# A two-layer graph transformer on one core: raw rows gathered in layer 2, and gathers that wait for the chunk two before

## The chip, the cores and the metric

One core of a Trainium2 chip runs the whole program in one launch. The metric is the time of one execution on the device in microseconds (us). A comparison gives the median of several runs; beside it one execution is recorded by the hardware profiler, and all stage times in this document are from such a record.

## The reference

A graph of N = 6250 nodes with D = 128 features and E = 106250 edges sorted by their target node. Two attention layers with 2 heads of 64, the same for both but for their weights:

```python
q, k, v = (h @ Wq + bq, h @ Wk + bk, h @ Wv + bv)         # per head
e = edge_attr @ We          # edge_attr: 64 message features and 32 cosines of a relative time
alpha = sum(q[dst] * (k[src] + e)) / 8
a = softmax of alpha over the edges of each target node
out = segment_sum((v[src] + e) * a, dst) + h @ Ws + bs
```

Between them h is normalised over the nodes (batch norm: mean and variance of each feature, then scale and shift), and a ReLU follows. Behind layer 2 the input x is added and each row goes through a layer norm.

## The kernel before, in words

**Chunks.** The edges are cut into 106 chunks of 1024 (8 tiles of 128), and a chunk's edges lead to at most 64 target nodes. `conv(c, extra)` works on them in a software pipeline: iteration k does different stages of chunks k+4 to k−2, written out by hand in a fixed order, and each engine keeps that order. `c` is 0 in layer 1 and 1 in layer 2.

**Rows.** For each chunk the source nodes' rows are gathered into a buffer `ff` (128 edges of a tile on the partitions, tiles side by side, followed by message features, time encoding and a few more columns). `gather(k)` (L751) issues 8 indirect DMAs of 128 rows each on GpSimd (POOL), which does nothing else in the loops. There are six such buffers, and in iteration k `fetch(k+4)` (plain loads on SP, and small DVE work) and `gather(k+4)` come first; so a chunk's gathers are issued four chunks ahead and wait only until the buffer of six chunks before is free.

**What happens to a chunk.** `turn_in` transposes its rows on TensorE (PE) in two halves (L805), and ScalarE (ACT) copies them from PSUM to `fft` (L812). All eight gathers of the chunk are awaited by its first transpose. In layer 1 the edge features are transposed too (L817, L818) and stored in `et_d` for layer 2; `encode` (L769 to L777) computes the time encoding on VectorE (DVE). `score` (L830, L831) multiplies with a table of the target nodes, `lowest` and `weigh` turn scores into exponentials (L837, L845), `turn_weights` transposes these (L855, L856), and `gather_sums` (L862) multiplies them with `ff`, which gives the weighted sums of rows and edge features, and the sum of weights in the last column. `divide` (L867 to L870), `finish_turn` (L882, L885), `apply` (L892 or L898, L899) and `finish` (L909 or L922 on) make the layer's output from these sums. The value and edge weights are applied to the sums, not to each edge; the table holds what the keys need.

**Extra work.** `pull(extra)` runs one or two steps of other work in each iteration: the tables of later blocks of 512 nodes (L629 to L639), and in layer 2 the residual of each block (L1085 to L1095). At the end of layer 1 it also turns finished blocks of h into rows and writes them to `h_d` (L1027, L1029, L1037), and takes their moments.

**Between the layers.** The moments give `scale` and `shift` (L1067 to L1076). Block 0 of h goes through the ReLU and gets its table. Then `conv(1, ...)` starts, and its first iteration calls `first_blocks`: the ReLU of the other twelve blocks in place (L1106), then each block is turned into rows again (49 transposes, 13 DVE copies) and written to a second table, `hn_d`. The first RAW = 3 chunks gather from `h_d`, raw, for which `fft` is made with a ReLU activation with scale and shift (L810) and `normalise` repairs `ff` in place with three DVE operations (L875, L876) before its sums; the other 103 chunks gather normalised rows from `hn_d`.

## Time and profile before

| | us |
|---|---|
| median of 3 runs | 2755.56 (2752.11 to 2757.98) |
| the profiled execution | 2730.3 |
| its span on the core | 2728.4 |
| PE busy in the span | 2340.9 (86%) |
| POOL busy | 1619.5 (59%) |
| DVE busy | 1342.3 (49%) |
| ACT busy | 1241.6 (46%) |
| mean granted TensorE clock | 0.952 |

The page shows the span of the profiled execution; what the execution takes beyond it lies before the first and behind the last instruction. Busy shares are means over stages: the preparation (to about 38 us, the first gather), layer 1 (to about 1390 us), the step between the layers and layer 2. In the timelines a row is one instruction, or several of one kind in a row (their count is behind the `x`); "remote" as the end of an idle time stands for something the record doesn't show. The bracket of a gather names what its queue waited for, "issue" that it waited for nothing visible.

### The profile page before, as it was taken

The page shows a single profiled execution, that of the slowest core. Times are in us where ns is not written, and L with a number is a line of the kernel's source. Part 1 is how long each engine was busy: PE and PEld are TensorE (multiplying, and loading weights), DVE is VectorE, ACT ScalarE, POOL GpSimd, SP SyncE. Part 2 cuts the span into 40 slices and gives each one's busy share as a digit, 9 for nine tenths or more (in the row PEclk, how much of TensorE's full clock was granted, in tenths as well). Part 3 has the DMA queues.
Part 4 walks back from the last instruction along what each step waited for, and adds up shares of the span by engine and source line. Part 5 has one row for each costly group of instructions (what it writes and reads, how often), then busy time and mean ns, then how long its engine had stood idle before and what let it go on. Part 6 is the DMA issues. An engine that isn't in the chain of part 4 may idle for free. (4 is left out here: it accounts for less than half of the span.)

```text
span 2728.4 us, 39114 instructions
## 1 busy us (share of the span) xinstructions
PE 2340.9 (86%) x11586; PEld 1725.5 (63%) x11586; DVE 1342.3 (49%) x4162; ACT 1241.6 (46%) x2167; POOL 1619.5 (59%) x1717
## 2 busy tenths in 40 slices
PE   5599999999898989888957998888898888888887
PEld 3366666767676767666734665666666666666655
DVE  5366666666666666666634333333333333333333
ACT  2366666665555555445522343333334333333344
POOL 3466666566666666666335666666666666666660
PEclk7799999999999999999978999998999999999998
DMA  6255555545555455555436554555555555544440
GB/s 205 80 177 145 154 164 149 150 131 161 160 151 158 130 163 154 142 150 149 119 106 175 157 154 144 147 156 155 152 153 142 159 151 152 156 135 129 137 135 27
DMA packets 241161, 396.59 MB, mean 145 GB/s; under 512 B 62609, under 2 KB 158094, under 8 KB 237614
## 3 DMA queue, kind: packets, MB, share of 16 engines
q1 hardware_dynamic: 167728, 239.73, 29.5%
q0 software_dynamic: 54656, 113.07, 16.2%
q10 hardware_dynamic: 18558, 41.20, 4.3%
q8 instruction: 98, 1.61, 0.2%
q14 instruction: 121, 0.99, 0.1%
HBM read 277.19 MB, written 113.17 MB: 143 GB/s over the span
## 5 line engine op out<-in xcount | busy, mean ns | idle before, releaser
L751 POOL DMA_INDIRECT ff<-xv_d,fsrcs x848 | 810.1, 955 | 512.8 <-issue 213.0
L751 POOL DMA_INDIRECT ff<-hn_d,fsrcs x824 | 782.2, 949 | 458.8 <-issue 208.7
L812 ACT COPY fft<-fpx 128x512 f32<-128x512 f32 x418 | 246.1, 589 | 1150.2 <-remote 439.9
L862 PE MATMUL fpa<-ff,fpt 128*128 128x225 f32 x3392 | 684.2, 354 | 0.6 <-issue 0.6
L862 PEld LDWEIGHTS fpa<-ff,fpt 128*128 128x128 f32 x3392 | 628.6, 190 | 4.8 <-issue 1.3
L830 PE MATMUL fps<-fft,ftab 128*128 128x512 f32 x848 | 480.4, 650 | 65.5 <-ACT fft L812 45.8
L837 DVE TENSOR_REDUCE flow<-fps 128x1 f32<-128x512 f32 x424 | 285.4, 686 | 455.5 <-PE fpx L805 124.5
L855 PEld LDWEIGHTS fppt<-fident,fs 128*128 128x128 f32 x1696 | 203.4, 145 | 145.2 <-issue 76.4
L856 ACT COPY fpt<-fppt 128x512 f32<-128x512 f32 x424 | 229.4, 585 | 108.8 <-PE fppt L855 47.5
L845 ACT ACTIVATE fs<-fps,fm 128x512 f32<-128x512 f32 x424 | 269.1, 689 | 4.8 <-DVE fm L839 2.1
L805 PE MATMUL fpx<-fident,ff 128*128 128x128 f32 x1696 | 259.3, 276 | 5.3 <-issue 1.1
L830 PEld LDWEIGHTS fps<-fft,ftab 128*128 128x128 f32 x848 | 168.0, 233 | 126.6 <-ACT fft L812 68.2
L855 PE MATMUL fppt<-fident,fs 128*128 128x128 f32 x1696 | 234.6, 282 | 11.6 <-ACT fft L810 5.4
L831 PE MATMUL fps<-fxT,ftab 112*128 112x512 f32 x424 | 236.8, 642 | 2.8 <-DMA fxT<-et_d 2.8
L831 PE MATMUL fps<-fet,ftab 112*128 112x512 f32 x424 | 221.0, 603 | 11.2 <-issue 11.2
L805 PEld LDWEIGHTS fpx<-fident,ff 128*128 128x128 f32 x1696 | 203.4, 142 | 34.8 <-issue 22.7
L817 PE MATMUL fpe<-fident,ff 128*112 128x128 f32 x848 | 133.4, 281 | 72.6 <-ACT fft L812 69.7
L831 PEld LDWEIGHTS fps<-fet,ftab 112*128 112x128 f32 x424 | 106.8, 252 | 91.0 <-issue 88.9
L831 PEld LDWEIGHTS fps<-fxT,ftab 112*128 112x128 f32 x424 | 90.7, 214 | 116.3 <-issue 111.0
L885 DVE COPY fat<-fpo 128x256 f32<-128x256 f32 x212 | 89.2, 421 | 138.9 <-remote 58.9
L817 PEld LDWEIGHTS fpe<-fident,ff 128*112 128x112 f32 x848 | 95.8, 136 | 88.9 <-ACT fft L812 83.3
L818 ACT COPY fet<-fpe 112x512 f32<-112x512 f32 x212 | 127.4, 601 | 45.1 <-remote 16.0
(203 smaller groups left out, 2402.4 us busy)
## 6 DMA issues: line engine op xcount, KB each, us to landing
fmsg<-in_edge_attr SPq DMA_DIRECT2D x212, 256.0 KB
et_d<-fet SPq DMA_DIRECT2D x106, 448.0 KB
fxT<-et_d SPq DMA_DIRECT2D x106, 448.0 KB
ftab<-tab_d SPq DMA_DIRECT2D x106, 192.0 KB
tab_d<-fo ACTq DMA_DIRECT2D x13, 1536.0 KB
ff<-xv_d,fsrcs POOLq DMA_INDIRECT x848
enc_d<-fzs SPq DMA_DIRECT2D x106, 128.0 KB
ftab<-tab_d SPq DMA_DIRECT2D x106, 128.0 KB
```

The costliest lines, as they stand in the source:

```text
L751: nc.gpsimd.indirect_dma_start(out=f[:, t, (1 if c else 0):1 + D], out_offset=None, in_=(h_d if k < RAW else hn_d) if c else pl.xv_d, in_o ...
L805: turn = nc.tensor.transpose(px[:, t * P:(t + 1) * P], s.f[:, u * 4 + t, 1:1 + D], ident)
L812: nc.scalar.copy(s.ft[:, u * GE:(u + 1) * GE], px)
L817: nc.tensor.transpose(pe[:EC, t * P:(t + 1) * P], s.f[:, u * 4 + t, 1 + D:], ident)
L818: nc.scalar.copy(s.et[:, u * GE:(u + 1) * GE], pe[:EC])
L830: nc.tensor.matmul(ps, s.tab[:, :, 0], s.ft[:, w], start=True, stop=False)
L831: nc.tensor.matmul(ps, s.tab[:EC, :, 1], s.et[:, w], start=False, stop=True)
L837: nc.vector.tensor_reduce(low[:, u:u + 1], s.ps[u], AX.X, OP.min)
L845: nc.scalar.activation(s.s[:, u * GE:(u + 1) * GE], s.ps[u], AF.Exp, bias=s.bias, scale=-1.0)
L855: nc.tensor.transpose(pp[:, t * P:(t + 1) * P], s.s[:, at:at + P], ident)
L856: nc.scalar.copy(s.pt[:, u * GE:(u + 1) * GE], pp)
L862: nc.tensor.matmul(s.pa, s.pt[:, t * P:(t + 1) * P], s.f[:, t, 1:1 + D + EW], start=t == 0, stop=t == T - 1)
```

## The change

1. `hn_d` and `first_blocks` are gone. All chunks of layer 2 gather raw rows from `h_d`, and `fft` is always made with the ReLU activation (L810).
2. `normalise(k)` runs for each chunk of layer 2, behind `finish_turn(k - 2)`, with two operations: multiply by the scale, and take the larger of that and minus the shift. That is the normalised row less the shift. As the weights of a node's edges add up to one, the missing shift is the same for each node after the division; its product with the value weights is added once to the last row of the edge weights `web[1]`, which meets the column of ones.
3. The ReLU of a block is done in `block(b0)`, when its table is made.
4. Gathers are paced. Chunks 0 and 1 are gathered at once. Chunk 2 waits for the second half of the transposes of chunk 0; chunk j from 3 on is issued behind the first half of the transposes of chunk j − 2 and waits for the last of these. In layer 1 that holds to chunk NEAR = 30; chunk 31 follows chunk 30 directly, and from 32 on gathers come at the start of an iteration, four chunks ahead, as before. In layer 2 it holds to the end.

```diff
-    RAW = 3
+    NEAR = 30
...
-        def gather(k):
+        def gather(k, step=None):
             f = ch[k].f
-            ch[k].rows = [
+            rows = ch[k].rows = [
                 nc.gpsimd.indirect_dma_start(
-                    out=..., in_=(h_d if k < RAW else hn_d) if c else pl.xv_d,
+                    out=..., in_=h_d if c else pl.xv_d,
...
+            if step is not None:
+                tc.add_manual_dep(rows[0].ins, step.ins.name, together, reason="gathers keep to the pace of the chunks")
...
-                turn = nc.tensor.transpose(px[:, t * P:(t + 1) * P], s.f[:, u * 4 + t, 1:1 + D], ident)
+                turn = s.step = nc.tensor.transpose(px[:, t * P:(t + 1) * P], s.f[:, u * 4 + t, 1:1 + D], ident)
...
-            if c and k < RAW:
+            if c:
                 nc.scalar.activation(s.ft[:, u * GE:(u + 1) * GE], px, AF.Relu, bias=pl.shift, scale=pl.scale)
...
         def normalise(k):
             rows = ch[k].f[:, :, 1:1 + D]
-            for i, op in enumerate((OP.mult, OP.add)):
+            for i, op in enumerate((OP.mult, OP.max)):
                 nc.vector.tensor_tensor(rows, rows, pl.spread[:, None, i].to_broadcast([P, T, D]), op)
-            nc.vector.tensor_scalar(rows, rows, 0.0, None, op0=OP.max)
...
                 if on(k + AHEAD):
                     fetch(k + AHEAD)
-                    gather(k + AHEAD)
-                if k == -AHEAD and c:
-                    first_blocks()
+                    if c == 0 and k + AHEAD > NEAR + 1:
+                        gather(k + AHEAD)
...
                 if on(k - 2):
                     finish_turn(k - 2)
+                if c and on(k):
+                    normalise(k)
                 if on(k + 1):
                     turn_in(k + 1, 0)
+                if on(k + 3) and k != -1 and (c or k + 3 <= NEAR):
+                    gather(k + 3, ch[k + 1].step if on(k + 1) else None)
+                    if c == 0 and k + 3 == NEAR:
+                        gather(k + 4)
                 if on(k - 1):
                     gather_sums(k - 1)
...
                 if on(k + 1):
                     turn_in(k + 1, 1)
+                if k == -1:
+                    gather(2, ch[0].step)
...
                 if c and on(k):
-                    if k < RAW:
-                        normalise(k)
                     nc.vector.tensor_copy(ch[k].f[:, :, 1 + D:1 + D + TD], ch[k].z)
...
         def block(b0):
+            r = slice(b0 * GE, (b0 + 1) * GE)
+            nc.scalar.activation(hT[:, r], hT[:, r], AF.Relu, bias=shift, scale=scale)
             res = residual(b0)
...
+            below = const.tile([P, 1], F32, name="fbelow")
+            nc.vector.tensor_scalar(below, shift, -1.0, None, op0=OP.mult)
...
-            for i, col in enumerate((scale, shift)):
+            for i, col in enumerate((scale, below)):
...
+            last = const.tile([P, P], F32, name="flast")
+            nc.vector.memset(last, 0.0)
+            nc.vector.tensor_copy(last[:, P - 1:], shift)
+            pw_ = pp.tile([P, P], F32, name="fpb", bufs=1)
+            nc.tensor.matmul(pw_, last, wv[1], start=True, stop=True)
+            nc.vector.tensor_add(web[1], web[1], pw_)
```

More of the change, by code (lines that the diff above doesn't have):

```diff
@@ L675, in ordered @@
     h_d = dram.tile([N, D], F32, name="h_d")
-    hn_d = dram.tile([N, D], F32, name="hn_d")
     at_round = [0]
@@ L697, in ordered, with conv @@
     SINGLE = 40
-    RAW = 3
-    def conv(c, extra, first_blocks=None):
+    NEAR = 30
+    def conv(c, extra):
         cs = ExitStack()
@@ L746, in fetch @@
                 nc.sync.dma_start(s.r, res_d[bass.ds(s.nb, NN), :])
-        def gather(k):
+        def gather(k, step=None):
             f = ch[k].f
-            ch[k].rows = [
+            rows = ch[k].rows = [
                 nc.gpsimd.indirect_dma_start(
-                    out=f[:, t, (1 if c else 0):1 + D], out_offset=None, in_=(h_d if k < RAW else hn_d) if c else pl.xv_d,
+                    out=f[:, t, (1 if c else 0):1 + D], out_offset=None, in_=h_d if c else pl.xv_d,
                     in_offset=bass.IndirectOffsetOnAxis(ap=pl.srcs[:, t, k:k + 1], axis=0))
                 for t in range(T)]
+            if step is not None:
+                tc.add_manual_dep(rows[0].ins, step.ins.name, together, reason="gathers keep to the pace of the chunks")
         shape = [P, T, TD]
@@ L1102, in block @@
             yield
-        def relu(b0):
-            r = slice(b0 * GE, (b0 + 1) * GE)
-            nc.scalar.activation(hT[:, r], hT[:, r], AF.Relu, bias=shift, scale=scale)
-        def first_blocks():
-            for b0 in range(1, NT):
-                relu(b0)
-            for b0 in range(-(-N // GE)):
-                put_rows(hn_d, b0, turned_rows(b0))
         with tc.tile_pool(name="fpp2", bufs=3, space=bass.MemoryType.PSUM) as pp, tc.manual_schedule():
             pl.bank = lambda: pp.tile([P, GE], F32, name="fpg")
-            relu(0)
             for _ in block(0):
@@ L1133, in rest @@
                 yield
-        conv(1, rest(), first_blocks)
+        conv(1, rest())
     nc.sync.dma_start(out[N - NN:N, :], tail_d[NN:2 * NN, :])
```

## The prediction

> **What bounds the kernel now.** I read the first part of the page, then the costliest groups, and then went stage by stage through the timelines of POOL, ScalarE (ACT) and TensorE (PE). The columns of a timeline row are start, time taken, engine, line, operation, and in brackets the idle time before it and what ended that.
>
> ```profile
> span 2728.4 us, 39114 instructions
> PE 2340.9 (86%) x11586; PEld 1725.5 (63%) x11586; DVE 1342.3 (49%) x4162; ACT 1241.6 (46%) x2167; POOL 1619.5 (59%) x1717
> L751 POOL DMA_INDIRECT ff<-xv_d,fsrcs x848 | 810.1, 955 | 512.8 <-issue 213.0
> L751 POOL DMA_INDIRECT ff<-hn_d,fsrcs x824 | 782.2, 949 | 458.8 <-issue 208.7
> ```
>
> PE is busy for 86% of the span, which looks like a bound. The rounds of single chunks say something narrower. Four starts of the first feature copy where no gather is running (two late in layer 1, two late in layer 2):
>
> ```profile
> 1342.62 0.58 ACT L812 COPY fft<-fpx 128x512 f32<-128x512 f32 x1 [1.77 <-PE fpx L805]
> 1352.52 0.58 ACT L812 COPY fft<-fpx 128x512 f32<-128x512 f32 x1 [1.80 <-PE fpx L805]
> 2682.12 0.58 ACT L812 COPY fft<-fpx 128x512 f32<-128x512 f32 x1 [0.57 <-PE fpx L805]
> 2691.41 0.58 ACT L812 COPY fft<-fpx 128x512 f32<-128x512 f32 x1 [1.75 <-PE fpx L805]
> ```
>
> PE needs 9.9 us for a chunk in layer 1 and 9.3 us in layer 2. While gathers run a chunk takes longer. By POOL's busy time and its number of gathers in two long stretches:
>
> ```profile
> 156.00:1316.00 1160.00, 729.72 (x764) 0.99 0.51 151
> 1520.00:2604.00 1084.00, 690.37 (x728) 0.96 0.52 148
> ```
>
> 764 gathers are 95.5 chunks of 8: 12.15 us a chunk in layer 1; 728 are 91 chunks: 11.91 us in layer 2. One round of layer 2 on three engines shows why:
>
> ```profile
> 1915.51 0.94 POOL L751 DMA_INDIRECT ff<-hn_d,fsrcs  x1 [2.19 <-PE fpo L899]
> 1924.24 0.94 POOL L751 DMA_INDIRECT ff<-hn_d,fsrcs  x1 [0.30 <-issue]
> 1927.42 0.94 POOL L751 DMA_INDIRECT ff<-hn_d,fsrcs  x1 [2.24 <-PE fpo L899]
> 1920.46 0.60 PE L805 MATMUL fpx<-fident,ff 128*128 128x128 f32 x4
> 1927.08 0.58 ACT L812 COPY fft<-fpx 128x512 f32<-128x512 f32 x1 [7.19 <-PE fpo L899]
> ```
>
> The first and last of eight gathers start at 1915.51 and 1924.24. PE's transposes are over at 1921.06, yet ACT copies them only at 1927.08, 6 us later, and POOL goes on 0.34 us after that. So in a run of gathers the other engines learn late what PE has done, and catch up when the run has been served: 1927.08 − 1915.51 = 11.57 us for 8, 1.45 us a gather. Two longer runs give the same, at the start of the kernel and between the layers:
>
> ```profile
> 38.71 0.96 POOL L751 DMA_INDIRECT ff<-xv_d,fsrcs  x1 [27.93 <-DVE fbits L734]
> 97.82 0.94 POOL L751 DMA_INDIRECT ff<-xv_d,fsrcs  x1 [0.30 <-issue]
> 106.25 0.59 ACT L812 COPY fft<-fpx 128x512 f32<-128x512 f32 x1 [20.77 <-remote]
> 120.45 0.98 POOL L751 DMA_INDIRECT ff<-xv_d,fsrcs  x1 [21.68 <-PE fpa L862]
> 1392.58 0.94 POOL L751 DMA_INDIRECT ff<-h_d,fsrcs  x1 [58.93 <-DVE fshift L1076]
> 1425.54 2.02 DVE L1029 COPY fhr<-fpg 128x512 f32<-128x512 f32 x3 [5.60 <-remote]
> 1439.10 0.94 POOL L751 DMA_INDIRECT ff<-hn_d,fsrcs  x1 [16.86 <-DMA hn_d<-fhr]
> 1473.34 0.78 ACT L810 ACTIVATE fft<-fpx,fshift,fscale 128x512 f32<-128x512 f32 x1 [8.67 <-remote]
> 1473.52 0.94 POOL L751 DMA_INDIRECT ff<-hn_d,fsrcs  x1 [4.32 <-remote]
> ```
>
> 48 gathers: 38.71 to 106.25, 1.41 us each. 24: 1392.58 to 1425.54, 1.37. 24 again: 1439.10 to 1473.34, 1.43. Gather service, 11.3 to 11.6 us a chunk, is what a round consists of; PE's 9.3 to 9.9 us lie inside it. Time is therefore lost where no gather is being served though some are left: 106.25 to 120.45 (14.2 us; the pipeline has only one chunk done, and all six row buffers are full), and 1425.54 to 1439.10 (13.6 us, waiting for the normalised table).
>
> **The change part by part.** *Start of layer 1.* Only chunks 0 and 1 are gathered at once: 16 × 1.41 = 22.6 us, served at 61.3. Chunk 2 then follows the transposes of chunk 0, and each later one a round. The 14.2 us gap is gone. Against it, chunks 2 to 5 now come in rounds of 12.15 instead of 8 × 1.41 = 11.28 us: 4 × 0.87 = 3.5 us. Gain 10.7 us. Chunk 31 goes right behind chunk 30 and from 32 on the old rule of four ahead holds; the two extra chunks gathered there hold the transposes up for about two rounds, but no gather is added and none is late, so layer 1's last gather stays 10.7 us early and the four chunks behind it cost what they cost now. In between, a gather is released by a transpose and not, as now, by a freed buffer:
>
> ```profile
> 192.90 0.98 POOL L751 DMA_INDIRECT ff<-xv_d,fsrcs  x1 [2.05 <-PE fpa L862]
> ```
>
> Here POOL waits for the sums (L862) that follow the first transposes in PE's order. A release by L805 can come earlier, by 0 to 0.3 us in each of 28 rounds (0 to +8 us); the other bound is that rows only two chunks ahead arrive late for the edge encoding, at most 0.5 us a round (−14 us). I take 0: what ended both kinds of wait above is the end of the same run. In layer 1 POOL has nothing but gathers, so only further gathers queue behind the new wait.
>
> *Between the layers.* The 15 writes to hn_d, the 49 transposes and 13 copies go, and with them the 16.86 us wait. After: chunks 0 and 1 from 1392.58, served 16 × 1.40 = 22.4 us later at 1415.0; chunks 2 to 5 in four rounds of 11.91 us, so chunk 6 starts at 1462.6 instead of 1473.52: 10.9 us early. The 12 ReLUs that ran together now come one with each block, on an ACT that has room (below). The few operations for the shift in the last weight row stand behind block 0; no gather waits for them, and the first user is the apply of chunk 0, two rounds later: nothing.
>
> *End of layer 2.* Now the last gather is four chunks ahead, after the change two. From
>
> ```profile
> 2662.32 0.94 POOL L751 DMA_INDIRECT ff<-hn_d,fsrcs  x1 [0.31 <-issue]
> 2665.22 0.58 ACT L812 COPY fft<-fpx 128x512 f32<-128x512 f32 x1 [5.89 <-remote]
> ```
>
> the last run is served at 2665.22, with chunk 102 just transposed; chunk 104 comes at 2682.12. After the change chunk 104 is the one transposed when the last run ends: 2682.12 − 2665.22 = 16.9 us saved. This is the same saving as the early start of chunks 0 and 1 seen from the other end: fewer chunks are left when the gathers are over.
>
> *Rounds of layer 2.* Each chunk now has ACT's ReLU in place of the copy, and two DVE operations:
>
> ```profile
> L812 ACT COPY fft<-fpx x418: 567/586/607, 56.4 to 2694.9; 128x512 f32<-128x512 f32 x140
> L810 ACT ACTIVATE fft<-fpx,fshift,fscale x6: 777/777/781, 1434.3 to 1473.3; 128x512 f32<-128x512 f32 x6
> L875 DVE TENSOR_TENSOR ff<-ff,fspread x6: 1220/1226/1226, 1447.1 to 1489.4; 128x1024 f32<-128x1024 f32 x6
> 1700.00:2000.00 300.00, 266.65 (x1311) 190.44 (x1311) 113.66 (x378) 113.74 (x243) 190.47 (x201) 0.95 0.54 153
> ```
>
> ACT: 206 × 0.19 = 39 us more work, DVE: 103 × 2.45 = 252 us more. Both are busy 38% of this stretch (third and fourth pair after the length: DVE 113.66, ACT 113.74 of 300), 4.5 of 11.9 us in a round, so there is room. The place matters: normalising stands behind the copy of the turned sums (L885) that PE waits for, and ahead of the message copy, the finish and the divide:
>
> ```profile
> 2005.23 0.42 DVE L788 COPY ff<-fmsg 128x512 f32<-128x512 f32 x1
> 2010.68 0.28 DVE L922 SCALAR_TENSOR_TENSOR fres<-fpo,fr 64x128 f32<-64x128 f32 x1 [5.03 <-PE fpg L629]
> ```
>
> DVE idles 5.03 us just there; 2.45 fit. Without that cover the divide would be late and a round longer by up to 2.45 us.
>
> *POOL beside normalising.* Here a gather is slowed:
>
> ```profile
> 1447.15 2.48 DVE L875 TENSOR_TENSOR ff<-ff,fspread 128x1024 f32<-128x1024 f32 x2
> 1447.82 1.37 POOL L751 DMA_INDIRECT ff<-hn_d,fsrcs  x1 [0.30 <-issue]
> ```
>
> 1.37 instead of 0.94: 0.43 us a chunk, at most two gathers so, 0.86. Whether that lengthens a round can be read where another operation stretched a run:
>
> ```profile
> 1998.95 1.05 POOL L751 DMA_INDIRECT ff<-hn_d,fsrcs  x1 [2.40 <-PE fpo L899]
> 2005.30 1.17 POOL L751 DMA_INDIRECT ff<-hn_d,fsrcs  x1 [0.30 <-issue]
> 2008.02 0.94 POOL L751 DMA_INDIRECT ff<-hn_d,fsrcs  x1 [0.30 <-issue]
> 2010.77 0.94 POOL L751 DMA_INDIRECT ff<-hn_d,fsrcs  x1 [1.81 <-PE fpg L629]
> ```
>
> Issuing took 10.01 us here (to 2008.96) against 9.67 in the round at 1915.51 (to 1925.18); the idle time behind it fell from 2.24 to 1.81 us, and the round is 11.82 against 11.91. The stretch was swallowed. I take 0, with bounds 0 and 0.86 × 103 = 89 us. The Trainium skill speaks against this change here: by "SBUF — State Buffer", section "SBUF: two separate sides", a DVE operation with two SBUF inputs and a GpSimd operation that reads SBUF share a port pair which one holds for its whole instruction while the other is fully blocked. By that rule POOL would lose whole operations, which is a rival below; the 0.43 us of the row bears out a loss, but a third of one operation only.
>
> *Sum.* 10.7 + 10.9 + 16.9 = 38.5 us. The span goes to 2690, the profiled execution from 2730.3 (span and 1.9 us around it) to 2692. The median of the timed runs, 2755.56, is 25 us above the profiled one; I take the same 39 us off: **2717 us**.
>
> **The rivals.** *Normalising stretches every round (slower).* If the stretch of the gathers does lengthen the rounds, 0.43 to 0.86 us a chunk cost 44 to 89 us: 2761 to 2806. It decides from 38.5 / 103 = 0.37 us a round. For it: the 1.37 us gather, and DVE taking 252 us more beside POOL. Against it: the swallowed 0.34 us above. Chance 0.17.
>
> *POOL held for the whole of both operations (slower).* 2.45 us a chunk, of which the idle time behind a run (2.24 us) swallows all it has or nothing: 0.2 to 2.45 us, 103 times, 21 to 252 us on top of 2717: 2738 to 2969. Against it: the gather beside the operations would then take 0.94 + 1.23 = 2.17 us, not 1.37. Chance 0.04. This is what the port rule of the Trainium skill's "SBUF — State Buffer" gives.
>
> *Paid back.* Two chunks ahead may be too few: where a round is late, PE now waits for rows at once, where four chunks in buffers hid it. A run served 11.57 us after its release leaves one round before its own transposes, so up to 0.3 us a round over 130 rounds could go, 0 to 39 us: 2717 to 2756; around 2737. Chance 0.15, a third of it near no change.
>
> *Tighter rounds.* With gathers released by the transposes, rounds could come down from 11.9 towards the 11.3 us of service: 0.3 us × 131 rounds (28 and 103) = 39 us more, 2678. For it: layer 1's 12.15. Against: in layer 2 POOL already restarts 0.34 us behind the copy of the transposes. Chance 0.12.
>
> *The change doesn't do what it says.* If the late news from PE had another cause than the gathers, the starts would crawl as now, and only the 16.9 us at the end and hn_d's wait, 13.6 us, would move, in either direction: within 15 us of before. Chance 0.06.
>
> **How the numbers follow.** The forecast case (2695 to 2735 by itself) has 0.46. A measurement of this kernel can tell about 0.2%, 5.5 us, from no change. Faster: 0.46, 0.12 from the tighter rounds, 0.10 from what is paid back, 0.03 from the last case: 0.71. Within 0.2%: 0.05, the rest of what is paid back. Slower: 0.17 + 0.04 + 0.03 = 0.24. The range leaves out half of the tighter rounds (0.06), the far part of the first rival (0.09) and most of the second (0.03): 2677 to 2785.
>
> **What would show it.** Right: POOL's first idle stretch near 55 us instead of 98.8, and 8 gathers a round from there; no gather waiting on a table after 1392; chunk 3 of layer 2 copied near 1451 (chunk 0 at 1415 and three rounds of 11.9); two copies of features behind the last gather; rounds of 11.9 us in layer 2 with POOL's idle time down from 2.2 to about 1.8 us. Wrong: rounds of 12.3 us or more in layer 2; gathers beside the DVE operations at 1.8 us or more; PE idle ahead of L805 for rows; a stall near chunk 30 that is longer than 23 us.

## The result and the profile after

The changed kernel is slower: 2823.48 us against 2755.32, a ratio of 1.0246 (95% interval 1.0217 to 1.0275), 68 us. The prediction said 2717 us, 39 us faster.

The numbers below need one thing said first. The kernel before itself takes about 2310 us in four of the six sessions of experiments (a session: runs made together on one chip) and 2727 or 2756 us in the other two; one and the same chip showed 2311 in one session and 2727 in another. All measured ratios are against the kernel before in the same session. I call the two conditions **prompt** and **late**, by what the traces show of them: in a prompt trace the first feature copy of a chunk starts 0.04 to 0.1 us behind its transposes, in a late one up to 6 us. The prediction and the result are both of the late condition. The trace of before (2730.3 us) is of a run 25 us faster than its median of 2755; the trace after (2827.3 us) lies near its median. So a comparison of the two traces shows some 29 us too much: their spans differ by 96.8 us, the medians by 68.

The page of after: first part and two groups.

```profile
span 2825.2 us, 39185 instructions
PE 2369.4 (84%) x11539; PEld 1757.7 (62%) x11539; DVE 1561.4 (55%) x4356; ACT 1299.6 (46%) x2167; POOL 1680.7 (59%) x1717
L750 POOL DMA_INDIRECT ff<-h_d,fsrcs x848 | 861.1, 1015 | 555.1 <-issue 217.4
L876 DVE TENSOR_TENSOR ff<-ff,fspread 128x1024 f32<-128x1024 f32 x212 | 258.9, 1221 | 4.9 <-issue 1.2
```

A gather of layer 2 takes 1015 ns on the mean instead of 949. The places that the prediction named, in the timelines of POOL and ACT after the change:

```profile
37.95 0.97 POOL L750 DMA_INDIRECT ff<-xv_d,fsrcs  x1 [26.85 <-DVE fbits L733]
65.69 0.99 POOL L750 DMA_INDIRECT ff<-xv_d,fsrcs  x1 [8.00 <-PE fpx L806]
101.97 0.59 ACT L813 COPY fft<-fpx 128x512 f32<-128x512 f32 x1
434.94 0.59 ACT L813 COPY fft<-fpx 128x512 f32<-128x512 f32 x1 [0.38 <-PE fpx L806]
469.22 0.59 ACT L813 COPY fft<-fpx 128x512 f32<-128x512 f32 x1 [9.33 <-remote]
1421.09 0.95 POOL L750 DMA_INDIRECT ff<-h_d,fsrcs  x1 [59.12 <-DVE fscale L1078]
1444.04 0.95 POOL L750 DMA_INDIRECT ff<-h_d,fsrcs  x1 [3.11 <-PE fps L832]
1479.52 0.78 ACT L811 ACTIVATE fft<-fpx,fshift,fscale 128x512 f32<-128x512 f32 x1 [1.80 <-PE fpx L806]
2780.43 0.78 ACT L811 ACTIVATE fft<-fpx,fshift,fscale 128x512 f32<-128x512 f32 x1 [0.29 <-PE fpx L806]
```

The starts went as forecast. Chunk 3 of layer 1 is copied at 101.97 instead of 131.86. In layer 2 the gathers of chunk 2 come 22.95 us behind the first (22.4 forecast), chunk 3 is copied 58.4 us behind it (58 forecast; 88.1 before). The return to four chunks ahead is the pause from 434.94 to 469.22, two to three rounds; from chunk 28 to chunk 30 it takes 46.4 us instead of 24.1, so 22.4 us more, which is near the two rounds that were forecast. What went wrong is the rounds. By the starts of the first copy of chunks 3 and 28, and of 10 and 96 in layer 2: 13.32 us a chunk in layer 1's paced part (12.07 before), 12.93 in layer 2 (11.92 before). 25 × 1.25 = 31 us and 86 × 1.01 = 87 us ate up everything.

The same can be told by the gathers. The first gather of layer 2 starts 28.5 us later than before (1421.09 against 1392.58): in layer 1 the lead of 30 us at chunk 3 was spent on the longer rounds (31 us) and on the pause (22.4 us). From there to the last gather (2777.26 against 2662.32) it takes 86.4 us more, and what follows the last gather is 18.2 us shorter. Together that is 96.7 us, the difference of the two traces.

### The profile page after: what moved, and what is told of

Same layout as the page of the kernel before. It is cut to its first block, busy times and chain, and to the rows that moved or that the text cites. A ratio compares the mean times of both kernels' runs of the same rounds, so it can differ in the third digit from the quotient of the medians.

```text
span 2825.2 us, 39185 instructions
## 1 busy us (share of the span) xinstructions
PE 2369.4 (84%) x11539; PEld 1757.7 (62%) x11539; DVE 1561.4 (55%) x4356; ACT 1299.6 (46%) x2167; POOL 1680.7 (59%) x1717
## 5 line engine op out<-in xcount | busy, mean ns | idle before, releaser
L750 POOL DMA_INDIRECT ff<-h_d,fsrcs x848 | 861.1, 1015 | 555.1 <-issue 217.4
L863 PE MATMUL fpa<-ff,fpt 128*128 128x225 f32 x3392 | 743.5, 375 | 86.0 <-ACT fpt L857 61.3
L863 PEld LDWEIGHTS fpa<-ff,fpt 128*128 128x128 f32 x3392 | 670.6, 203 | 111.0 <-ACT fpt L857 68.2
L831 PE MATMUL fps<-fft,ftab 128*128 128x512 f32 x848 | 466.6, 633 | 26.6 <-ACT fft L811 13.8
L811 ACT ACTIVATE fft<-fpx,fshift,fscale 128x512 f32<-128x512 f32 x212 | 165.4, 780 | 439.2 <-remote 221.1
L813 ACT COPY fft<-fpx 128x512 f32<-128x512 f32 x212 | 125.1, 590 | 451.8 <-PE fpx L806 265.1
L806 PE MATMUL fpx<-fident,ff 128*128 128x128 f32 x1696 | 265.8, 281 | 16.9 <-ACT fxT L655 8.8
L876 DVE TENSOR_TENSOR ff<-ff,fspread 128x1024 f32<-128x1024 f32 x212 | 258.9, 1221 | 4.9 <-issue 1.2
L832 PE MATMUL fps<-fxT,ftab 112*128 112x512 f32 x424 | 227.5, 618 | 0.6 <-issue 0.4
```

Source lines behind the costliest of these rows:

```text
L750: nc.gpsimd.indirect_dma_start(out=f[:, t, (1 if c else 0):1 + D], out_offset=None, in_=h_d if c else pl.xv_d, in_offset=bass.IndirectOffs ...
L806: turn = s.step = nc.tensor.transpose(px[:, t * P:(t + 1) * P], s.f[:, u * 4 + t, 1:1 + D], ident)
L811: nc.scalar.activation(s.ft[:, u * GE:(u + 1) * GE], px, AF.Relu, bias=pl.shift, scale=pl.scale)
L831: nc.tensor.matmul(ps, s.tab[:, :, 0], s.ft[:, w], start=True, stop=False)
L832: nc.tensor.matmul(ps, s.tab[:EC, :, 1], s.et[:, w], start=False, stop=True)
L863: nc.tensor.matmul(s.pa, s.pt[:, t * P:(t + 1) * P], s.f[:, t, 1:1 + D + EW], start=t == 0, stop=t == T - 1)
```

## The experiments

Theories: **A**, a gather run released by the transposes starts at a place of PE's order that makes the rounds long; **B**, two chunks of lead are too few, and something waits for rows; **C**, normalising slows the gathers, by its two inputs in SBUF (port) or just by DVE's time (occupancy).

All runs of parts 1 and 2 fell into the prompt condition. What raw_only, no_norm, late_release and relu_first were expected to show is told in microseconds of the late one; so of these expectations only the direction can be compared, whether a theory makes the rounds longer or shorter.

**1. Parts alone (prompt).**

raw_only, without the pacing:

```diff
-                    if c == 0 and k + AHEAD > NEAR + 1:
-                        gather(k + AHEAD)
+                    gather(k + AHEAD)
...
-                if on(k + 3) and k != -1 and (c or k + 3 <= NEAR): ...
-                if k == -1: gather(2, ch[0].step)
```

> Parts 1 to 3 of the change without the pacing: raw rows and normalising in all of layer 2, ReLU with the block's table, but every chunk's gathers issued at the start of an iteration, four chunks ahead, as in the kernel before. If the place at which a gather run is released makes the rounds long (theory A: a run now starts ahead of the sums in PE's order, so the hand-overs of the next iteration fall into the time in which the other engines hear late of PE), layer 1 is that of before to a few us (chunk 105's first feature copy at 1362 +- 5 us against 1392 after the change), layer 2 runs at 11.9 to 12.2 us a chunk, and the whole is 2745 to 2785. If normalising is what makes rounds long (theory C), layer 2 stays at 12.7 us or more and the whole is 2820 or more. If two chunks of lead are too few (theory B), as under A.

no_norm, without normalising, so that the sums of layer 2 are of raw rows:

```diff
-                if c and on(k):
-                    normalise(k)
```

> The changed kernel with the two DVE operations that normalise the gathered rows of layer 2 left out (so the sums of layer 2 are made of raw rows). Theory A: layer 1 unchanged, layer 2 falls from 12.85 us a chunk to 12.5 at the lowest; whole 2785 to 2825. Theory C: layer 2 at 11.9 to 12.0 us a chunk, whole 2730 to 2740. Gathers of layer 2 go from 1015 ns on the mean back to about 950 under both.

late_release, the block of `gather(k + 3, ...)` moved:

```diff
                 if on(k + 1):
                     turn_in(k + 1, 1)
+                if on(k + 3) and k != -1 and (c or k + 3 <= NEAR):
+                    gather(k + 3, ch[k + 1].step if on(k + 1) else None)
```

> The changed kernel with the gathers of chunk k+3 issued behind the second half of the transposes of chunk k+1 and waiting for the last of these: the same two chunks of lead, but released some 3.9 us later in PE's order, behind the sums. Theory A: layer 1's paced rounds (chunks 3 to 28) go from 13.3 us back to 12.1, layer 2 from 12.85 to 12.0 to 12.4; whole 2715 to 2765. Theory B (too short a lead: PE waits for rows): the lead is 3.9 us shorter still, so rounds grow, 13.3 us or more in layer 1, and the whole is 2850 or more.

relu_first, the ReLUs together at k = −4 of layer 2:

```diff
+                if k == -AHEAD and c:
+                    first_blocks()      # for b0 in range(1, NT): relu(b0)
```

> The changed kernel with the ReLU of the twelve blocks done together at the start of layer 2, as before, instead of one with each block. In the trace after the change PE's table products (L629) waited 32.7 us for that ReLU in eight places of layer 2. If those waits are on the path, the whole is 20 to 33 us shorter: 2790 to 2805. If they only stand where another wait would (theory A), 0 to 10 us: 2813 to 2824.

after_again, before_again: the two kernels as they are. 

> The changed kernel once more, beside the experiments. The last four kernels ran on a chip on which the kernel before takes 2312 us and no engine hears late of PE (the first feature copy of a chunk starts 0.04 to 0.1 us behind its transposes); the two traces of before and after are from one with 2755 us. On a chip like the first the changed kernel should be at 1.018 to 1.021 of before, as the same kernel with its ReLUs first is at 1.020; on a chip like the second at 1.022 to 1.028.

> The kernel before, for its trace on the chip of the experiments. On the chip with 2312 us PE should be busy for some 95% of the span, rounds of 10.6 to 10.7 us in layer 1 and 10.0 to 10.1 in layer 2 (there 12.15 and 11.91 on the other chip), and feature copies within 0.1 us of their transposes; a start that crawls (chunk 3 copied later than 120 us) would speak against the late news as its cause.

start_only, pacing to chunk 6 in both layers:

```diff
-    NEAR = 30
+    NEAR = 6
-                    if c == 0 and k + AHEAD > NEAR + 1:
+                    if k + AHEAD > NEAR + 1:
-                if on(k + 3) and k != -1 and (c or k + 3 <= NEAR):
+                if on(k + 3) and k != -1 and k + 3 <= NEAR:
...
-                    if c == 0 and k + 3 == NEAR:
+                    if k + 3 == NEAR:
```

> The changed kernel with the pacing only to chunk 6 in both layers; from chunk 8 on gathers come at the start of an iteration, four chunks ahead. Theory A (the place of release makes rounds long): rounds behind chunk 8 are those of gathers four ahead, and what is left is normalising; on a chip with 2312 us 1.010 to 1.014 of before (raw rows without pacing had 1.0127), on a chip with 2755 us 0.99 to 1.005. If raw rows and normalising are what costs there, 1.015 or more on the chip with 2755 us.

three_ahead:

```diff
-                    if c == 0 and k + AHEAD > NEAR + 1:
+                    if c == 0 and k + AHEAD > NEAR:
...
-                if on(k + 3) and k != -1 and (c or k + 3 <= NEAR):
-                    gather(k + 3, ch[k + 1].step if on(k + 1) else None)
-                    if c == 0 and k + 3 == NEAR:
-                        gather(k + 4)
+                if on(k + 4) and k != -1 and (c or k + 4 <= NEAR):
+                    gather(k + 4, ch[k + 1].step if on(k + 1) else None)
...
-                    gather(2, ch[0].step)
+                    gather(3, ch[0].step)
```

> The changed kernel with the gathers one chunk further ahead: chunk j waits for the transposes of chunk j - 3, issued at the same place in the iteration. Theory B (two chunks of lead are too few, PE or the encoding waits for rows): paced rounds of layer 1 come down to those of unpaced gathers, and the whole by 10 to 20 us where before takes 2312, by 40 to 90 us where it takes 2755. Theory A: the run is released at the same place, rounds stay within 0.1 us, the whole within 10 us of the changed kernel.

pace_only, the kernel before with the pacing of the changed one (the lines of the change that pace gathers, and no others):

> The kernel before (normalised table, first blocks, three raw chunks) with the pacing alone, in both layers as in the changed kernel. Where before takes 2312 us the changed kernel's layer 1 ended 12 us later than before, so 1.005 at least; layer 2 rounds as in no_norm, 10.05 us against 9.93: 1.005 to 1.012. Where before takes 2755 us: theory A 1.015 or more (rounds of 13.3 us in layer 1's paced part, 12.5 or more in layer 2); if normalising was all, 1.00 to 1.01.

Ratio to before, and rounds from the starts of the feature copies (layer 1: chunks 3 to 28; layer 2: 10 to 96), and the gathers' mean from the groups of the page (for before_again and pace_only, of the gathers from `hn_d`):

| kernel | ratio (interval) | layer 1, us | layer 2, us | gather of layer 2, ns |
|---|---|---|---|---|
| before_again | 1 | 10.51 | 9.93 | 954 |
| after_again | 1.0211 (1.0183 to 1.0240) | 10.87 | 10.33 | 993 |
| raw_only | 1.0127 (1.0111 to 1.0144) | 10.51 | 10.38 | 997 |
| no_norm | 1.0052 (1.0035 to 1.0069) | 11.00 | 10.06 | 947 |
| pace_only | 1.0103 (1.0085 to 1.0121) | 11.01 | 10.02 | 955 |
| late_release | 1.0432 (1.0408 to 1.0456) | 12.61 | 10.38 | 994 |
| relu_first | 1.0198 (1.0180 to 1.0216) | 10.88 | 10.43 | 999 |
| start_only | 1.0140 (1.0117 to 1.0162) | 10.58 | 10.36 | 995 |
| three_ahead | 1.0142 (1.0122 to 1.0163) | 10.51 | 10.35 | 995 |

So the change costs 2.1% in the prompt condition too, and there two causes can be told apart.

*Pacing, layer 1.* It costs 0.36 to 0.50 us a round. With the gathers a chunk further ahead, released at the same place, it costs nothing; released 3.9 us later it costs 2.1 us a round. That is theory B, and against A. The first to wait is not PE but the time encoding. Waits of DVE, chunks 3 to 28, before_again, after_again and late_release (columns: waiter, what ended it, us in total, times, longest):

```profile
DVE flow L837 <- PE fps L831: 26.5, 26, 1.4
```

```profile
DVE frel L770 <- issue: 38.5, 17, 4.8
DVE frel L770 <- DMA ff<-xv_d,fsrcs: 7.9, 5, 1.9
```

```profile
DVE frel L770 <- DMA ff<-xv_d,fsrcs: 66.0, 17, 6.7
DVE frel L770 <- issue: 31.7, 8, 6.0
```

`encode(k + 2)` begins with L770, which reads a column of the gathered rows, and stands one iteration behind their release; neither before_again nor three_ahead has a wait there. (Where the record names what ended these waits, it is the landing of a gather; "issue" means that it names nothing.) Behind it in DVE's queue stands the divide, and for that PE waits. The waits of PE in the same stretch, after_again and late_release; before_again has none:

```profile
PE fpo L882 <- DVE fa L871: 5.3, 6, 2.0
```

```profile
PE fpo L882 <- DVE fa L871: 34.4, 20, 3.8
```

That is 5.3 of the 9 us that after_again loses in these 25 rounds, and 34.4 of late_release's 52. In layer 2 the pacing costs 0.09 us a round by itself (pace_only) and nothing that can be told where gathers are stretched too (after_again against raw_only).

*Raw rows, layer 2.* raw_only has no pacing, and its layer 1 runs as that of before_again, but in layer 2 a round takes 10.38 us against 9.93. What happens to a gather is seen in POOL's timeline, of before_again and of raw_only; for raw_only each of two passes of normalising stands ahead of the gathers beside it:

```profile
1963.89 0.94 POOL L751 DMA_INDIRECT ff<-hn_d,fsrcs  x1 [0.30 <-issue]
1965.14 0.94 POOL L751 DMA_INDIRECT ff<-hn_d,fsrcs  x1 [0.30 <-issue]
1966.38 0.94 POOL L751 DMA_INDIRECT ff<-hn_d,fsrcs  x1 [0.30 <-issue]
```

```profile
1965.47 2.48 DVE L876 TENSOR_TENSOR ff<-ff,fspread 128x1024 f32<-128x1024 f32 x2
1964.86 0.95 POOL L750 DMA_INDIRECT ff<-h_d,fsrcs  x1 [0.30 <-issue]
1966.11 1.40 POOL L750 DMA_INDIRECT ff<-h_d,fsrcs  x1 [0.30 <-issue]
1967.81 0.95 POOL L750 DMA_INDIRECT ff<-h_d,fsrcs  x1 [0.31 <-issue]
1273.54 2.48 DVE L876 TENSOR_TENSOR ff<-ff,fspread 128x1024 f32<-128x1024 f32 x2
1273.60 1.97 POOL L750 DMA_INDIRECT ff<-h_d,fsrcs  x1 [0.30 <-issue]
1275.88 0.96 POOL L750 DMA_INDIRECT ff<-h_d,fsrcs  x1 [0.30 <-issue]
```

A pass is two operations of 1.22 us each. The first ends at 1966.69 in the one pass and at 1274.76 in the other, and the gather that started while it ran ends 0.82 us behind that, at 1967.51 and 1275.57. This holds throughout: in raw_only's layer 2, 96 gathers start in a first operation (from 0.02 us behind its start to 0.13 us before its end), and each of them ends 0.81 to 0.83 us behind that end, however early it started. So a gather is held until the operation is over, and what it loses is decided by when it starts: from nothing to 1.06 us (2.0 us instead of 0.95), 0.40 us on the mean of the passes. The second operation costs hardly anything. The gather behind the held one starts some 0.13 us before that operation's end, and takes 0.95 to 0.96 us.

Why the stretch is not swallowed: POOL has no idle time left in either kernel. Undisturbed gathers follow each other 1.25 us apart, 8 × 1.25 = 10.0 us a chunk. In before_again that is level with PE, which is busy for 789 of 795 us in these rounds (a round can be 9.93 us because the gathers begin with a lead: from the last gather's end to the chunk's first copy it is 15.9 us at chunk 10 and 3.7 at chunk 96); in raw_only the 8 gathers take 10.38 us, and so does the round. PE's waits at the transposes in layer 2, of before_again and of raw_only:

```profile
PE fpx L805 <- issue: 9.5, 6, 2.3
```

```profile
PE fpx L806 <- issue: 35.0, 26, 3.8
PE fpx L806 <- DMA ff<-h_d,fsrcs: 3.9, 2, 2.0
```

By the gathers' means, 8 × (997 − 954) ns are 0.34 us of the 0.45.

What raw rows gain between the layers is there: from the last chunk of layer 1 to chunk 10 of layer 2, 162.5 us before, 147.7 in raw_only, 150.0 in after_again.

**2. Port or occupancy (prompt).**

psum_norm, the spread scale and bound read from PSUM (the diff of psum_bank is the same, with a bank of its own):

```diff
+            pa_all = p_a.tile([P, GE], F32, name="fpa")
+            spread_p = pa_all[:, 256:].rearrange("p (i d) -> p i d", d=P)
...
-                nc.vector.tensor_tensor(rows, rows, pl.spread[:, None, i].to_broadcast([P, T, D]), op)
+                nc.vector.tensor_tensor(rows, rows, spread_p[:, None, i].to_broadcast([P, T, D]), op)
```

> Raw rows without pacing (as raw_only), but scale and minus shift, spread over the partitions, lie in PSUM, in the unused half of the bank of the sums, so the two DVE operations have one input in SBUF and one in PSUM. In raw_only gathers of layer 2 took 1.40 to 1.47 us beside those operations, POOL had no idle time left there, and a chunk took 10.38 us against 9.93 before. If it is the two SBUF inputs that slow the gathers (theory C, port), the gathers of layer 2 go back to about 950 ns on the mean, a chunk to 9.9 to 10.05 us, and the whole is 0.990 to 0.999 of before where before takes 2312 us. If it is DVE's time, whatever its inputs (theory C, occupancy), 1.010 to 1.015 as raw_only.

max_only, one operation:

```diff
-            for i, op in enumerate((OP.mult, OP.max)):
-                nc.vector.tensor_tensor(rows, rows, pl.spread[:, None, i]...
+                nc.vector.tensor_tensor(rows, rows, pl.spread[:, None, 1].to_broadcast([P, T, D]), OP.max)
...
+            nc.vector.tensor_scalar(wv[1], wv[1], scale, None, op0=OP.mult)
```

> Raw rows without pacing, with one DVE operation a chunk in place of two: the larger of the raw row and minus shift over scale; the scale goes into the rows of the value weights once (the scale is positive here). Both inputs in SBUF. Port or occupancy: half of raw_only's price in layer 2, 0.2 to 0.25 us a chunk, 1.000 to 1.005 of before where before takes 2312 us. If the price is fixed for each chunk and not for each operation: 1.010 or more.

psum_bank:

```diff
-        p_s = ...(tc.tile_pool(name=f"fp_s{c}", bufs=3, ...
+        p_s = ...(tc.tile_pool(name=f"fp_s{c}", bufs=3 - c, ...
+            p_n = cs.enter_context(tc.tile_pool(name="fp_n", bufs=1, space=bass.MemoryType.PSUM))
+            spread_p = p_n.tile([P, 2, P], F32, name="fspreadp")
```

> As psum_norm, but scale and minus shift have a PSUM bank to themselves (the scores of layer 2 have two banks instead of three), since in psum_norm PE's sums (L866) waited 318 us for the normalising that read from their bank, while the gathers beside it were back at 944 ns. If the two SBUF inputs are what slows gathers, and gather issue is what bounds layer 2 on a chip with 2312 us: gathers of layer 2 at 950 ns on the mean, 9.9 to 10.1 us a chunk, 0.990 to 1.000 of before. If two score banks are too few, PE waits ahead of L831 show it, with 950 ns gathers. If it is DVE's time: 1.010 to 1.016.

raw_spread, the kernel before with RAW = 12:

```diff
-    RAW = 3
+    RAW = 12
+                if c and -1 <= k < 6:
+                    first_blocks(k + 1)      # two blocks turned and written
```

> The kernel before with twelve raw chunks instead of three, and the turning and writing of the normalised table not at the start of layer 2 but two blocks in each of the iterations -1 to 5. This keeps what raw rows gain between the layers (15 to 17 us earlier at chunk 10 in raw_only and start_only, where before takes 2312) and pays normalising for 12 chunks only (12 x 0.45 = 5 us), but the 49 transposes and 13 copies still have to be done (5 us of PE). 0.995 to 1.000 where before takes 2312 us, 0.988 to 1.000 where it takes 2755. If raw rows cost something else than normalising, 1.005 or more.

raw_only_2: as raw_only.

> Raw rows without pacing once more, beside the two others. Where before takes 2312 us: 1.011 to 1.015 as the first time. Where it takes 2755: theory A (release of paced gathers is what makes rounds long there) 0.995 to 1.010; if normalising costs there what it costs on the other chips, 0.4 to 0.5 us a chunk, less some 27 us between the layers, also within these; 1.015 or more would say that pacing is not what costs there.

| kernel | ratio (interval) | layer 2, us | gather of layer 2 |
|---|---|---|---|
| psum_norm | 1.2218 (1.2200 to 1.2236) | 14.95 | 944 ns median, 1150 at most |
| max_only | 1.0129 (1.0114 to 1.0145) | 10.34 | 996 ns mean |
| psum_bank | 0.9972 (0.9960 to 0.9983) | 9.99 | 952 ns mean |
| raw_spread | 1.0050 (1.0036 to 1.0063) | 9.94 | 991 ns mean of the raw, 957 of the others |
| raw_only_2 | 1.0130 (1.0115 to 1.0146) | 10.40 | 998 ns mean |

psum_norm says nothing of the price: the constants share a bank with the sums, and PE's sums waited for each pass that read them (the first line of its PE waits):

```profile
PE fpa L866 <- DVE ff L879: 318.0, 98, 3.6
```

psum_bank settles it. Same two operations, same place, same 1.22 us each, one input in PSUM; the group of gathers and a pass with the gathers beside it:

```profile
L753 POOL DMA_INDIRECT ff<-h_d,fsrcs x848 | 807.4, 952 | 313.8 <-issue 223.0
1963.02 2.46 DVE L879 TENSOR_TENSOR ff<-ff,fspreadp 128x1024 f32<-128x1024 f32 x2
1963.54 0.95 POOL L753 DMA_INDIRECT ff<-h_d,fsrcs  x1 [0.30 <-issue]
1964.79 0.95 POOL L753 DMA_INDIRECT ff<-h_d,fsrcs  x1 [0.30 <-issue]
```

No gather is held: 0.95 us beside both operations, 9.99 us a chunk instead of 10.38, and the kernel is 0.28% faster than before, 38 us faster than raw_only. It is the two SBUF inputs and not DVE's time. The Trainium skill ("SBUF — State Buffer", section "SBUF: two separate sides") has exactly this condition, and its rule that the other engine fully blocks for the whole instruction agrees with raw_only's trace, where the gathers end 0.82 us behind the operation, whatever their own start. max_only's miss fits that: one operation costs nearly what two cost (0.41 us a round of 0.45), since in a pass of two the second holds hardly anything up; there too each of the 91 gathers that start within an operation ends 0.81 to 0.83 us behind it.

raw_spread missed: PE waited 19.0 us for the divide (L882 for `fa`, 13 times; 6.9 us in before_again) between the layers, as twelve passes of three operations and thirteen copies now stand in DVE's queue at once.

**3. The late condition.**

paced_psum: the changed kernel with psum_bank's constants. start_psum: psum_bank with start_only's pacing.

> The changed kernel, pacing and all, with scale and minus shift in a PSUM bank of their own as in psum_bank. It leaves the price of the pacing alone. If the two causes add, layer 1 ends 12 us later than in psum_bank (as after_again against before_again), layer 2 at 10.0 us a chunk: 1.001 to 1.006 of before where before takes 2312 us. If pacing hid or brought part of the price of normalising, layer 2 above 10.15 us a chunk and 1.008 or more. Where before takes 2755 us: 1.015 or more if pacing is what costs there, 1.000 to 1.010 if normalising is.

> psum_bank with the pacing kept to chunk 6 in both layers (as start_only). Where before takes 2312 us the start of layer 1 gained 0.1 us by it and layer 2 nothing, so as psum_bank to 0.2%: 0.995 to 0.999. Where before takes 2755 us the gap behind the first 48 gathers (14 us) and its like between the layers go: 0.975 to 0.990. This is the version that should beat both kernels on either chip.

l1_start: the kernel before with pacing to chunk 6 in layer 1 only. start_psum_relu: start_psum with relu_first's ReLUs.

> The kernel before, with its layer 2 untouched, and only layer 1 paced, to chunk 6. In start_psum this brought layer 1 to its end 15 us earlier where before takes 2727 us, and nothing (0.1 us) where it takes 2311 us. So 0.993 to 0.997 of before on the first, 0.998 to 1.002 on the second. If what is gained at the start is given back later, 0.998 or more on the first too.

> start_psum with the ReLU of the twelve blocks at the start of layer 2, as before. Where before takes 2727 us PE waited 36.6 us in nine places of start_psum's layer 2 for the ReLU in front of a block's products; if that is on the path, 0.990 to 0.997 of before there (start_psum was 1.0036), and if PE then waits as long for something else, 1.001 to 1.005. Where before takes 2311 us the same waits are 9.5 us in ten places: 0.990 to 0.998, psum_bank having 0.9972.

| kernel | before in its session, us | ratio (interval) | layer 1, chunks 3 to 28 | layer 2, us |
|---|---|---|---|---|
| (the changed kernel) | 2755 | 1.0246 (1.0217 to 1.0275) | 13.32 | 12.93 |
| paced_psum | 2727 | 1.0125 (1.0104 to 1.0147) | 12.50 | 12.48 |
| start_psum | 2727 | 1.0036 (1.0021 to 1.0052) | | 12.26 |
| l1_start | 2756 | 0.9981 (0.9970 to 0.9991) | | 12.09 |
| start_psum_relu | 2756 | 0.9958 (0.9944 to 0.9972) | | 12.15 |

(Where pacing ends at chunk 6, the pause for the two extra chunks lies within chunks 3 to 28, and no round is given.) l1_start's layer 2 is that of the kernel before, so 12.09 is the mark of that session; the trace of before, with 11.92, is of a faster one. Against the mark 12.93 is 0.84 us more: 0.45 goes with the second SBUF input (12.93 to 12.48, as in the prompt condition), 0.22 with the pacing (to 12.26). The rest is near what the sessions differ by.

paced_psum fell between its two expectations: of the changed kernel's 2.5% about half is left when the second SBUF input is gone. Not all of that can be the input's doing. Layer 1 is the same program in both, and its last chunk was copied at 1391.88 us in the changed kernel's trace and at 1362.20 in paced_psum's. For layer 2 the direct sign is in the gathers, 1015 ns on the mean against 952, 8 × 63 ns = 0.50 us a chunk. In the changed kernel's trace, too, a gather that starts during an operation ends 0.82 us behind it:

```profile
1468.38 2.48 DVE L876 TENSOR_TENSOR ff<-ff,fspread 128x1024 f32<-128x1024 f32 x2 [0.51 <-issue]
1468.48 1.95 POOL L750 DMA_INDIRECT ff<-h_d,fsrcs  x1 [0.30 <-issue]
```

But POOL still stood idle for 2.4 us a round there, beyond the 0.30 us between two gathers. That the stretch lengthens a round by all of its length in the late condition is likely by these numbers, and not shown.

start_psum missed by 1.4% to 2.9%, in two ways. Its rounds are long, with PE waiting for the ReLU and for the exponentials in front of the second score bank (its waits of PE, 1529 to 2600 us):

```profile
PE fps L834 <- ACT fs L849: 66.7, 41, 4.0
PE fpg L629 <- ACT fhT L1109: 36.6, 9, 5.8
```

With the ReLUs first (start_psum_relu) the second line is gone, and the kernel goes from 0.4% slower to 0.4% faster than before. The wait for the exponentials is left; whether a third score bank would save it was not tried, and paced_psum, with two as well, doesn't have it:

```profile
PE fps L834 <- ACT fs L849: 55.0, 49, 2.8
```

And the start of layer 1 is worth 5 us (l1_start), not 15: against the trace of before it leads by 29.5 us at chunk 3 and by 5.1 at chunk 6, when the two extra chunks have been gathered. start_psum_relu is the best kernel measured in the late condition, psum_bank in the prompt one; neither was measured in the other.

## Why the prediction was wrong

- **The gaps at both starts**: right in mechanism and size, in the late condition. There are 30 us of lead at chunk 3 in layer 1, chunk 2 of layer 2 at 22.95 us, chunk 3 at 58.4. In the prompt condition there is nothing to gain in layer 1: six chunks gathered at once, and chunk 1 is copied at

```profile
64.19 0.59 ACT L812 COPY fft<-fpx 128x512 f32<-128x512 f32 x1 [0.30 <-PE fpx L805]
```

 not at 106.25. So the crawl is no property of 48 gathers as such, but of the condition, and the 1.41 us of "service" are the late condition's.

- **The end of layer 2**: right. The last gather starts at 2777.26 and chunk 104, last but one, is copied at 2780.43 (its row is above); from the last gather's start to the end of the span it is 47.9 us instead of 66.1, 18.2 less (16.9 forecast):

```profile
2777.26 0.94 POOL L750 DMA_INDIRECT ff<-h_d,fsrcs  x1 [0.30 <-issue]
```

- **"I take 0" for the encoding's rows** (bounds 0 and 0.5 us a round, 28 rounds): the first failed step. In the prompt condition the term is 0.36 to 0.50 us a round, shown by DVE's waits at L770, and gone with one chunk more of lead. In the late condition, for which the forecast was made, paced rounds were 0.4 to 1.25 us longer than 12.07, up to two and a half times the bound, but this wait is not the reason: DVE waited at L770 for 2.1 us in all. PE waited for the copy of the turned weights and for the divide instead (0 and 3.2 us before). The changed kernel, chunks 3 to 28:

```profile
PE fpe L818 <- ACT fpt L857: 15.9, 11, 2.8
PE fpo L882 <- DVE fa L871: 15.2, 10, 3.1
DVE frel L770 <- issue: 2.1, 3, 1.2
```

 Why these two come late is not shown. The rival "paid back" had the cause half right for the prompt condition, too short a lead, but put the wait at PE's transposes instead of at DVE.

- **"I take 0" for the stretched gathers** (bounds 0 and 0.86 us a chunk): the second failed step, and the larger one. In the prompt condition it is 0.45 us a chunk, the row's own 0.43 us: some 39 us over 86 chunks. In the late one the gathers were stretched by 0.50 us a chunk, and rounds were 0.45 us shorter without the second SBUF input. One round in which 0.34 us were swallowed, after another operation, was taken for the rule. The first rival had the price (0.43 to 0.86) and the point from which it decides (0.37); it got 0.17. Its time alone, 2761 at the lower end, falls short of 2823, as the paced rounds of layer 1 cost too.

- **The rival of two whole operations** was turned down by a misread row. The gather at 1447.82 took only 1.37 us because it started 0.67 us into the operation; it ended at 1449.19, 0.81 us behind the operation's end at 1448.38. Only a gather that starts together with the operation shows the whole of it, and those took up to 2.0 us (raw_only) and 1.98 (the changed kernel), beyond the 1.8 us that the prediction named as a sign of being wrong. So POOL is held for the whole of one operation, as this rival said. Its price of 2.45 us a chunk was still wrong: a gather that starts within the operation loses only what is left of it, and the second operation holds hardly anything up.

- **ReLU at nothing** "on an ACT that has room": 9.5 us of PE waits in the prompt condition and no measurable time (relu_first 1.0198 to after_again's 1.0211). In the late one it is the 0.8% between start_psum and start_psum_relu, which differ in nothing else but ran in two sessions. ACT has room, but PE's table products stand right behind the ReLU. In the changed kernel's own layer 2 PE waited for it as follows; what that cost the kernel was not measured:

```profile
PE fpg L629 <- ACT fhT L1104: 32.7, 8, 12.4
```

- **The divide behind normalising**: right in the prompt condition, where PE's waits for `fa` in layer 2 stayed at 2.7 us in after_again and 3.0 in before_again. In the late trace they went from 1.2 to 23.8 us. Normalising alone does not bring that: start_psum normalises too, with pacing to chunk 6 only, and has 1.8 us; paced_psum, with all of the pacing, has 28.9.

- **PE is not the bound**: true of the late trace only. In the prompt one PE is busy for 96% of the span (before_again), and gather issue and PE are level.

What stays open is, first, what the late condition is; the same chip had both. Second, how 13.32 us in layer 1's paced rounds come about there: in paced_psum the same layer 1 ran at 12.50, so the size isn't stable. The two causes are shown by experiment for the prompt condition, in which the change costs 2.1%; for the 2.5% of the late one they are shown in part. That releasing a run ahead of the sums puts the next iteration's hand-overs into the time in which the other engines hear late of PE (theory A) was only argued; the prompt runs speak against the place as a cause, and no run with another place was made in the late condition.

## What to carry to other kernels

When a change adds an operation beside the engine that issues gathers, look at several gathers and at where in the operation each of them starts: one row of 1.37 us hid gathers of 2.0. Then multiply the mean loss by the rounds; a stretch that one round swallowed is not proof that all do, least of all if the issuing engine is level with the bound. Here a DVE operation with two SBUF inputs beside GpSimd's gathers became free of that price when its small operand went to PSUM, in a bank that nobody else writes. And a lead shortened on purpose has to be counted for every reader of the data: in the prompt condition the first reader was not the transposes but a small subtraction on DVE.

## What was not expected of the hardware

A gather of 128 rows, 0.95 us by itself, that starts during a DVE operation with two SBUF inputs ends 0.82 us behind that operation's end, in 96 of 96 cases of raw_only's layer 2; with one of the inputs in PSUM it takes 0.95 us (psum_bank).

The same kernel on the same chip took 2311 us in one session and 2727 in another, at a granted clock of 0.98 and 0.95 (psum_norm had 0.92 in a prompt session, so the clock is no mark of the condition). In the slower one ACT and DVE go on up to 6 us behind PE's work in a round with gathers, and with 48 gathers at once chunk 1 was copied at 106 us instead of 64. A tuning for the one condition is worth little in the other: pacing the start gained 5 us in the late one (l1_start), and brought layer 1 to its end 0.1 us earlier in the prompt one (start_only).
